# B-products of one state group moved from VectorE to GpSimd in the second layer's scans

## The chip, the cores and the metric

The kernel runs on one core of a Trainium2 chip. The metric is the device time of one execution in microseconds (us), from three runs of the kernel before: 15410.49 median, 15405.36 to 15414.3. A separate execution was recorded by the hardware profiler. The profile names the engines PE (TensorE, matrix products), DVE (VectorE), ACT (ScalarE), POOL (GpSimd) and SP (SyncE, which here only issues DMAs).

## The reference

Four layers run one after another on images of 64 x 64 tokens with 96 channels, four images in a batch. The first two are state-space layers with selective scans; the third (attention) and the fourth (Fourier mixing) and the feed-forward parts lie outside this change. The second layer's scan is, cut to what matters:

```python
def ss2d_core(xc, ...):                      # xc: 4 images, 192 channels, 4096 tokens
    xs = stack([x_hw, x_wh]); xs = concatenate([xs, flip(xs)])    # 4 directions
    dts, Bs, Cs = split(einsum(xs, x_proj_w), ...)                # 16 states
    delta = softplus(einsum(dts, dt_projs_w) + dt_projs_b)
    A = -exp(A_logs)
    def step(hst, inp):
        x_t, d_t, B_t, C_t = inp
        dA = exp(d_t[..., None] * A)
        hst = hst * dA + (d_t * x_t)[..., None] * B_t[:, :, None, :]
        y = einsum('bkdn,bkn->bkd', hst, C_t)
        return (hst, y)
    _, ys = scan(step, h0, seq)                                   # over 4096 tokens
```

So for every image, direction, channel and state there is one linear recurrence over 4096 tokens: the state is multiplied with a decay `dA` and the product `dt*x*B` is added. Then the states are weighted with `C` and summed. The first layer does the same with other scan orders (diagonals and radii), for which tokens are gathered.

## The kernel before, in words

**Tiling.** The 4096 tokens of a direction are cut into 4 segments of 1024. One image of one layer is a batch of 4 directions x 4 segments = 16 segments, which `Stream.batch` plans as one piece of work. Inside a segment the 192 channels x 16 states are cut into 24 groups: 6 channel blocks (`cb`) of 32 channels times 4 state groups (`sg`) of 4 states. A group is a tile of 128 partitions (32 channels x 4 states) by 1024 tokens.

**What happens to one group**, with the lines of the kernel before:
- `decay` (L1072, ScalarE): `da = exp(dts * A)`. `dts` is dt of the channel block, repeated over the states; it is loaded by a DMA that reads `dt_dram` with a broadcast (`load_dt`, L1056). `da` has 4 buffers in SBUF.
- `enter` (L1076, VectorE): `t = u * B`. `u` is dt*x of the channel block, repeated over the states by a matrix product into PSUM (`spread_u`, L1065, one buffer). `B` lies in SBUF in the tile `bc`, loaded per segment by broadcast DMAs (`load_states`, L1050). `t` has 2 buffers in PSUM.
- `recur` (L1083, VectorE): the scan, `h = da * h + t` along the tokens. `h` has 4 buffers in SBUF.
- `keep` (L1094, ScalarE): the last column of `h` is kept as the start of the next segment.
- `leave` (L1098, GpSimd): `hc = h * C`, with 3 buffers.
- `collect` (L1107, TensorE): sums `hc` over the states into PSUM; `keep_busy` (L1125) fills gaps of TensorE with products of zeros.

**Beside the groups** the planner lays the preparation of the next segment (`prepare`): tokens are transposed, projected to dt, B and C (L934, L947 to L951), dt goes through a softplus on ScalarE (an exponential and three passes, L991 to L995; the logarithm, L1006, with its table loads) and a sum on TensorE (L1014, L1017), is stored to `dt_dram` (L1020) and multiplied with x on GpSimd (`dtu`, L1023). B and C go through `bc_dram` (L981).

**What sets the order.** `batch` makes operations with an engine, a length, dependencies and due times, and `Flow.run` walks them once and emits each engine's instructions in a fixed order. Decay, product, scan and C-product are "hard": others may not be put before them if they would make them late. VectorE's order is written out: product, product, scan, scan for each pair of groups. Each engine then executes its instructions in order, waiting on semaphores, and SP issues the DMAs in order too, so a DMA that waits holds back those behind it.

**Between batches** `side_by_side` finishes an image (`merge`) while it prepares the next (`front`): these use temporaries `z_rows`, `xc`, `y_rows`, `yt`, `dx` and `halo`, taken from the pool `tmp` through `Rings`, a set of buffers that are taken and given back in turn.

Of the kernel before, what the change touches and what calls it, by code (L numbers as in the profile page):

```python
# [376 lines left out]
class Stream:  # L377
# [4 lines left out]
    def __init__(self, k, ctx, a, x, x1, y1):  # L382
# [20 lines left out]
        self.bc = k.t(w, [128, 2, NSG, SEG], "bc")  # L403
        self.zeros = k.t(w, [C, GC], "zeros")
        nc.gpsimd.memset(self.zeros, 0.0)

# [5 lines left out]
    def front(self, bt, plan, rings, first=None):  # L412
# [22 lines left out]
        def edges(s, st):  # L435

            halo = yield from take(self.tmp, [C, 2, HW], "halo", 2)
# [29 lines left out]
        def project(s, st):  # L467
# [31 lines left out]
            def outer(j):  # L499
# [6 lines left out]
                z = yield from take(self.tmp, [C, 2, CH], "z_rows", 2)  # L506
# [19 lines left out]
        def convolve(s, st):  # L526
            yield lambda: st.pad is not None
            xc = []
            for _ in range(C // GC):
                xc.append((yield from take(self.tmp, [128, CH], "xc", 3)))  # L530
# [26 lines left out]
            rows = yield from take(self.tmp, [128, 2, 4, DI], "y_rows", 1)  # L557
# [27 lines left out]
    def merge(self, bt, plan, rings):  # L585
# [29 lines left out]
        def times_d(n):  # L615

            x = yield from take(tmp, [128, T, DI], "dx", 1)
# [73 lines left out]
        def finish(n, acc, mv):  # L691
# [20 lines left out]
            yt = yield from take(tmp, [C, 2, CH], "yt", 1)  # L712
# [35 lines left out]
    def side_by_side(self, ahead, behind=None, flush=None, seg=None):  # L748
# [3 lines left out]
        plan, rings = Plan(), Rings(k)  # L752
        self.ended, self.idle = False, None
# [117 lines left out]
    def prepare(self, seg, base=0.0, before=None):  # L871
# [152 lines left out]

        for half in range(2):
# [17 lines left out]
            op(("u", half), "POOL", 2.31, partial(times, half), done, at=58.0 + 8.0 * half)  # L1043
# [13 lines left out]

    def spread_u(self, seg, cb):
# [10 lines left out]
    def decay(self, gr):  # L1069
        gr.da = self.k.t(self.core, [128, SEG], "da", bufs=4)  # L1070
        scale = gr.seg.bt.lay.neg_a[:, gr.seg.kd, gr.g : gr.g + 1]
        self.nc.scalar.activation(gr.da, gr.seg.dts[gr.cb], AF.Exp, scale=scale)  # L1072
# [5 lines left out]
    def recur(self, gr):  # L1078
# [6 lines left out]
        )  # L1085

# [97 lines left out]
    def batch(self, segs):  # L1184


        slot, length = 6.74, 6.74 * NCB * NSG / 2
        flow, last = Flow(self.keep_busy), segs[-1]
        add = flow.add
        groups = {}  # L1190
        dve = []
# [8 lines left out]
        for n, seg in enumerate(segs):  # L1200
            base, o, nxt = n * length, seg.o, seg.next
# [13 lines left out]
            for i in range(NG):  # L1215
                cb, sg = divmod(i, NSG)
                at = base + i // 2 * slot + i % 2 * 1.12
                gr = SimpleNamespace(seg=seg, cb=cb, sg=sg, g=i)
# [3 lines left out]
                if sg == 0:  # L1222
# [16 lines left out]
                    )  # L1239
                gr.decay = add(  # L1240
# [3 lines left out]
                    [o.get(("dts", cb)), of("recur", 4), of("decay", 1)],  # L1244
# [3 lines left out]
                gr.enter = add(  # L1248
                    "DVE",
                    1.115,  # L1250
                    partial(self.enter, gr),
                    [o["spread", cb], o.get(("load", 0, sg))],
                    lat=0.15,
                    due=at,
                    hard=True,
                )
                dve.append(gr)
# [1130 lines left out]
```

## Time and profile before

| what | value |
|---|---|
| median of three runs | 15410.49 us |
| the profiled execution's own time | 15402.95 us |
| its span, first to last instruction | 15401.2 us |
| granted TensorE clock, mean | 0.937 |
| VectorE busy over the span | 83% |
| GpSimd busy over the span | 60% |
| ScalarE busy over the span | 54% |
| second layer's batches and what lies between them, 6589 to 12195 us: VectorE / GpSimd / ScalarE busy | 5377 / 3936 / 3474 us of 5606 |

The page gives for each engine the busy time, then the span in 40 slices of 385 us with the busy share in tenths, then the costliest groups of instructions. A group's line reads: source line, engine, operation, tile written <- tiles read, shapes, count, then busy time and mean duration in ns, then how long the engine stood idle just before these instructions and which instruction's end released it. A timeline line reads: start, length, engine, line, operation, tiles, count of merged instructions, and in brackets the idle time before. Lines of waits read: who waited <- for whom: total us, times, longest.

### The profile page before, as it was taken

Reading aid. Unit: us, or ns where it says so; the run is one execution under the profiler, and the core shown is the slowest. Engines: PE = TensorE matmul, PEld = TensorE weight load, DVE = VectorE, ACT = ScalarE, POOL = GpSimd, SP = SyncE. Lnnn points to the kernel's source line nnn. Section 1 sums busy time; section 2 is a strip of 40 time slices with the busy share of each in tenths; the row PEclk is TensorE's granted clock in tenths of the full one; section 3 lists DMA queues with packets and bytes.
Section 4 is the critical chain, followed back from the end, with each engine's and each line's share of the span. In section 5 each row is a group of like instructions: output and inputs, shape, how many; then the busy total and the mean of one; then the engine's idle time right before and its main releaser. Section 6 shows DMA issues by size and latency. Waiting matters only on the chain. (4 is left out here: it accounts for less than half of the span.)

```text
span 15401.2 us, 196660 instructions
## 1 busy us (share of the span) xinstructions
PE 13827.4 (90%) x74369; PEld 5096.1 (33%) x74369; DVE 12827.4 (83%) x9642; ACT 8327.7 (54%) x13421; POOL 9203.3 (60%) x4657
## 2 busy tenths in 40 slices
PE   8899899989998999899989998999899789998877
PEld 3233333333333333333333333333233244443344
DVE  1999799978997899799979997999899856555655
ACT  3666466646664666466656665666566423232333
POOL 0788678867886688667747774777577620000123
PEclk9999899989998999899989999999999999998888
DMA  2333433343334333433343334333433400000122
GB/s 67 117 113 125 150 111 111 126 148 112 111 127 146 106 118 128 148 116 117 123 152 124 118 124 152 126 118 120 156 119 120 142 10 11 19 15 12 52 72 71
DMA packets 662768, 1637.49 MB, mean 106 GB/s; under 512 B 102822, under 2 KB 268460, under 8 KB 658045
## 3 DMA queue, kind: packets, MB, share of 16 engines
q1 hardware_dynamic: 624956, 1549.37, 31.4%
q0 software_dynamic: 36864, 75.55, 1.7%
q8 instruction: 588, 9.63, 0.3%
q14 instruction: 360, 2.94, 0.1%
HBM read 1295.03 MB, written 329.58 MB: 105 GB/s over the span
## 5 line engine op out<-in xcount | busy, mean ns | idle before, releaser
L1098 POOL TENSOR_TENSOR hc<-h,bc 128x1024 f32<-128x1024 f32 x3072 | 7198.4, 2365 | 2216.1 <-DVE h L1083 1909.0
L1083 DVE TENSOR_TENSOR_SCAN h<-da,state,t 128x1024 f32<-128x1024 f32 x2304 | 5300.4, 2355 | 26.0 <-ACT state L1094 16.3
L1072 ACT ACTIVATE da<-dts,L_A_logs 128x1024 f32<-128x1024 f32 x3072 | 3520.0, 1151 | 1832.2 <-DVE h L1083 1786.7
L1076 DVE TENSOR_TENSOR t<-u,bc 128x1024 f32<-128x1024 f32 x3072 | 3629.8, 1239 | 267.6 <-PE u L1065 193.5
L1107 PE MATMUL y<-hc,gather_y 128*32 128x512 f32 x12288 | 3529.1, 620 | 311.9 <-POOL hc L1098 241.7
L1125 PE MATMUL y<-L_diag,zeros 96*32 96x256 f32 x7824 | 1986.3, 386 | 0.0
L1083 DVE TENSOR_TENSOR_SCAN h<-da,t 128x1024 f32<-128x1024 f32 x768 | 1717.4, 2287 | 17.3 <-ACT da L1072 9.1
L1065 PE MATMUL u<-dtu,spread 32*128 32x512 f32 x3072 | 1573.1, 632 | 120.0 <-DVE t L1076 109.2
L1125 PEld LDWEIGHTS y<-L_diag,zeros 96*32 96x32 f32 x7824 | 852.8, 111 | 1425.0 <-issue 926.1
L1107 PEld LDWEIGHTS y<-hc,gather_y 128*32 128x32 f32 x12288 | 595.8, 109 | 2021.1 <-issue 1029.1
L934 PE MATMUL m<-xs,proj 96*128 96x512 f32 (+1 forms) x2048 | 1070.2, 641 | 67.3 <-ACT spare L1152 32.5
L1642 DVE SCALAR_TENSOR_TENSOR hcv<-padv,taps,hcv 128x2048 f32<-128x2048 f32 x384 | 902.2, 2350 | 13.4
L1566 POOL MEMSET padp<- 128x2448 f32 x32 | 68.6, 2143 | 1400.8 <-PE d L1606 1378.3
L1023 POOL TENSOR_TENSOR dtu<-dt,xs 96x1024 f32<-96x1024 f32 x256 | 603.0, 2356 | 506.1 <-ACT dt L1017 501.1
L1606 PE MATMUL d<-padp,diag 32*32 32x512 f32 x25600 | 885.7, 601 | 2.0 <-ACT hcp L1621 2.0
L1065 PEld LDWEIGHTS u<-dtu,spread 32*128 32x128 f32 x3072 | 521.4, 188 | 943.6 <-issue 588.0
L1017 ACT COPY dt<-m 96x512 f32<-96x512 f32 x512 | 297.2, 580 | 694.5 <-PE m L1014 690.0
L1014 PE MATMUL m<-dtu,ident 96*96 96x512 f32 x1024 | 563.8, 632 | 72.7 <-ACT dt L1017 65.9
L1606 PEld LDWEIGHTS d<-padp,diag 32*32 32x32 f32 x25600 | 484.4, 103 | 369.8 <-issue 196.9
L934 PEld LDWEIGHTS m<-xs,proj 96*128 96x128 f32 (+1 forms) x2048 | 324.6, 181 | 770.6 <-issue 483.8
L947 ACT ACTIVATE sp_z<-m,L_dtb 96x512 f32<-96x512 f32 x512 | 350.0, 684 | 409.5 <-PE m L934 393.5
L1014 PE MATMUL m<-sp_log,ident 96*96 96x512 f32 x1024 | 539.2, 608 | 0.0
(275 smaller groups left out, 15495.8 us busy)
## 6 DMA issues: line engine op xcount, KB each, us to landing
bc<-bc_dram SPq DMA_DIRECT2D x1024, 512.0 KB
dts<-dt_dram SPq DMA_DIRECT2D x768, 512.0 KB
dt_dram<-dt SPq DMA_DIRECT2D x256, 384.0 KB
y_tok<-spare SPq DMA_DIRECT2D x64, 768.0 KB
dt<-y_tok SPq DMA_DIRECT2D x128, 384.0 KB
x_tok<-y_rows SPq DMA_DIRECT2D x32, 768.0 KB
z_t<-z_rows SPq DMA_DIRECT2D x64, 384.0 KB
dx<-x_tok SPq DMA_DIRECT2D x64, 384.0 KB
```

Source lines behind the costliest of these rows:

```text
L934: nc.tensor.matmul(v.ps, seg.proj[:, src, to], seg.xs[:, src, chunks[j]], start=src == 0, stop=src == 1)
L1014: nc.tensor.matmul(v.ps, k.ident[:C, :C], term[:, half, chunks[j]], start=at == 0, stop=at == 3)
L1023: nc.gpsimd.tensor_mul(seg.dtu[:, half], v.dt[:, half], seg.xs[:, half])
L1065: self.nc.tensor.matmul(seg.u[:, cols], self.spread[rows, :], seg.dtu[rows, half, cols], start=True, stop=True)
L1072: self.nc.scalar.activation(gr.da, gr.seg.dts[gr.cb], AF.Exp, scale=scale)
L1076: self.nc.vector.tensor_mul(gr.t, gr.seg.u, self.bc[:, 0, gr.sg, :])
L1083: self.nc.vector.tensor_tensor_scan(gr.h[:, order], gr.da[:, order], gr.t[:, order], start, op0=ALU.mult, op1=ALU.add)
L1098: self.nc.gpsimd.tensor_mul(gr.hc, gr.h, self.bc[:, 1, gr.sg, :])
L1107: nc.tensor.matmul(seg.y[at : at + GC, :], self.gather_y, gr.hc[:, part * CH : (part + 1) * CH], start=gr.sg == 0, stop=gr.sg == NSG - 1, ...
L1125: self.nc.tensor.matmul(gr.seg.y[at : at + GC, :256], self.zeros, gr.seg.bt.lay.diag.rearrange("p h t c -> p (h t c)")[:, :256], start=Fal ...
L1606: nc.tensor.matmul(pc[i][j * 32 : (j + 1) * 32, :], diag[mine, ON_PE.index(t), tap, :], pad[mine, j * 8 + dy : j * 8 + dy + 8, dx : dx + H ...
L1642: nc.vector.scalar_tensor_tensor(to, win, wt, to, op0=ALU.mult, op1=ALU.add)
```

## The change

In the second layer (`lay.ordered` is false) the product with B of the third state group (`sg` = 2) in channel blocks 1 to 4 is computed by GpSimd. That is 4 of the 24 groups of a segment. GpSimd's operand is a copy of dt*x in SBUF: the preparation stores `dtu` to a DRAM tile `u_dram`, and a broadcast DMA (`load_u`) reads a channel block of it into a piece of a new SBUF tile `area`. GpSimd writes the product into another piece of `area` (`enter_pooled`). There are two pieces for copies and two for products. The decay of such a group is written by ScalarE into PSUM, into the buffer (tag `t`) that the group's own product would have taken; it is allocated behind the scan of the group two before. VectorE's order, which was product, product, scan, scan for all pairs, is product, scan, scan for a pair with such a group, and the due times follow that order. The decay of any other group now counts its 4 buffers over the groups that use them.

`area` has 7 x 1024 elements per partition. The temporaries of the stretches between batches named above become fixed pieces of it (`shared`), in the same rings.

```diff
+        self.area = k.t(w, [128, 7 * SEG], "area")
...
+        cut("z_rows", 2, C, h=2, t=CH)
+        cut("xc", 3, 128, t=CH)
+        cut("y_rows", 1, 128, f=2, t=4, d=DI)
+        cut("yt", 1, C, h=2, t=CH)
+        cut("dx", 1, 128, t=CH // 128, d=DI)
+        cut("halo", 2, C, e=2, w=HW)
...
-                z = yield from take(self.tmp, [C, 2, CH], "z_rows", 2)
+                z = yield from take(None, None, "z_rows", 2)
...
+        def u_out(half):
+            if half == 0:
+                seg.u_dram = k.t(self.dram, [2, C, SEG], "u_dram")
+            nc.sync.dma_start(seg.u_dram[half], seg.dtu[:, half])
...
+            if not lay.ordered:
+                op(("u_out", half), "SP", 0.1, partial(u_out, half), [p], at=60.0 + 8.0 * half, lat=3.0)
...
+    def load_u(self, gr):
+
+        gr.u = self.area[:, gr.pooled % 2 * SEG : (gr.pooled % 2 + 1) * SEG]
+        src = gr.seg.u_dram.rearrange("h c t -> (h c) t")[gr.cb * GC : (gr.cb + 1) * GC, :]
+        self.nc.sync.dma_start(gr.u, src.unsqueeze(1).to_broadcast([GC, GS, SEG]))
+
+    def enter_pooled(self, gr):
+        at = 2 + gr.pooled % 2
+        gr.t = self.area[:, at * SEG : (at + 1) * SEG]
+        self.nc.gpsimd.tensor_mul(gr.t, gr.u, self.bc[:, 0, gr.sg, :])
...
     def decay(self, gr):
-        gr.da = self.k.t(self.core, [128, SEG], "da", bufs=4)
+        if gr.pooled is None:
+            gr.da = self.k.t(self.core, [128, SEG], "da", bufs=4)
...
+        if gr.ahead:
+            gr.ahead.da = self.k.t(self.ps_t, [128, SEG], "t")
...
-        slot, length = 6.74, 6.74 * NCB * NSG / 2
+        pooled = lambda i: not segs[0].bt.lay.ordered and i % NSG == 2 and 0 < i // NSG < NCB - 1
+        order, times, at = [], {}, 0.0
+        for n in range(len(segs)):
+            for i in range(0, NG, 2):
+                order += [("enter", n, j) for j in (i, i + 1) if not pooled(j)]
+                order += [("recur", n, j) for j in (i, i + 1)]
+        for x in order:
+            times[x] = at
+            at += 1.12 if x[0] == "enter" else 2.25
...
+                if pooled(i):
+                    gr.pooled = len(theirs)
+                    theirs.append(gr)
+                    first = groups[n, i - 2]
+                    first.ahead, there = gr, [first.recur]
+                else:
+                    own.append(gr)
+                    there = [own[-5].recur] if len(own) > 4 else []
                 gr.decay = add(
                     "ACT",
                     1.05,
                     partial(self.decay, gr),
-                    [o.get(("dts", cb)), of("recur", 4), of("decay", 1)],
+                    [o.get(("dts", cb)), *there, of("decay", 1)],
...
+                if pooled(i):
+                    load = add(
+                        "SP",
+                        0.1,
+                        partial(self.load_u, gr),
+                        [theirs[-3].enter if len(theirs) > 2 else None, o.get(("u_out", cb // 3))],
+                        lat=4.5,
+                    )
+                    gr.enter = add(
+                        "POOL",
+                        2.31,
+                        partial(self.enter_pooled, gr),
+                        [load, o.get(("load", 0, sg)), theirs[-3].recur if len(theirs) > 2 else None],
+                        lat=0.2,
+                        hard=True,
+                    )
...
-        order = []
-        for j in range(0, len(dve), 2):
-            order += [dve[j].enter, dve[j + 1].enter, dve[j].recur, dve[j + 1].recur]
+        order = [groups[n, i].__dict__[kind] for kind, n, i in order]
```

## The prediction

> **What bounds the kernel now.** First the page: which engine is fullest, and where in the span.
>
> ```profile
> span 15401.2 us, 196660 instructions
> PE 13827.4 (90%) x74369; PEld 5096.1 (33%) x74369; DVE 12827.4 (83%) x9642; ACT 8327.7 (54%) x13421; POOL 9203.3 (60%) x4657
> ...
> DVE  1999799978997899799979997999899856555655
> ...
> POOL 0788678867886688667747774777577620000123
> ...
> L1098 POOL TENSOR_TENSOR hc<-h,bc 128x1024 f32<-128x1024 f32 x3072 | 7198.4, 2365 | 2216.1 <-DVE h L1083 1909.0
> L1083 DVE TENSOR_TENSOR_SCAN h<-da,state,t 128x1024 f32<-128x1024 f32 x2304 | 5300.4, 2355 | 26.0 <-ACT state L1094 16.3
> L1072 ACT ACTIVATE da<-dts,L_A_logs 128x1024 f32<-128x1024 f32 x3072 | 3520.0, 1151 | 1832.2 <-DVE h L1083 1786.7
> L1076 DVE TENSOR_TENSOR t<-u,bc 128x1024 f32<-128x1024 f32 x3072 | 3629.8, 1239 | 267.6 <-PE u L1065 193.5
> L1125 PE MATMUL y<-L_diag,zeros 96*32 96x256 f32 x7824 | 1986.3, 386 | 0.0
> ```
>
> VectorE is full in long stretches up to slice 32, broken by dips between batches. TensorE's 90% misleads: L1125 is its filler of zeros, and matmul ends are modelled. GpSimd and ScalarE idle mostly because they wait for VectorE's scan (1909 and 1787 us), so in the scans VectorE leads and the rest follow.
>
> Then the second layer alone. By the first product and the last scan in the timeline its four batches run from 6589 to 7891, 8051 to 9344, 9500 to 10801 and 10900 to 12195 us. First the waits of VectorE inside the first of them, then its timeline of two slots, then GpSimd's of the same kind:
>
> ```profile
> DVE t L1076 <- PE u L1065: 10.3, 15, 2.3
> DVE h L1083 <- ACT state L1094: 1.3, 1, 1.3
> ```
>
> ```profile
> 8504.72 2.38 DVE L1076 TENSOR_TENSOR t<-u,bc 128x1024 f32<-128x1024 f32 x2
> 8506.97 4.62 DVE L1083 TENSOR_TENSOR_SCAN h<-da,state,t 128x1024 f32<-128x1024 f32 x2
> 8511.46 2.39 DVE L1076 TENSOR_TENSOR t<-u,bc 128x1024 f32<-128x1024 f32 x2
> ```
>
> ```profile
> 8518.62 2.36 POOL L1023 TENSOR_TENSOR dtu<-dt,xs 96x1024 f32<-96x1024 f32 x1
> 8520.94 7.00 POOL L1098 TENSOR_TENSOR hc<-h,bc 128x1024 f32<-128x1024 f32 x3
> 8529.74 4.68 POOL L1098 TENSOR_TENSOR hc<-h,bc 128x1024 f32<-128x1024 f32 x2 [1.79 <-PE m L897]
> ```
>
> VectorE waits 11.6 us in 1290: it is the bound to 1%. Starts count here, not durations, which overlap by 0.12 us: two products take 8506.97 - 8504.72 = 2.25 us, so one is 1.125; two scans take 4.49; a slot of two groups is 6.74, and a segment of 12 slots 80.9. On GpSimd three in a row span 7.00, so one is (7.00 - 2.36) / 2 = 2.32 us. Its segment holds 24 C-products and 2 of dt*x, 26 x 2.32 = 60.3 us of 80.9: 20 us free.
>
> **The change, part by part.** The sum stands against the profiled execution, 15402.95 us (span 15401.2 and 1.8 around it); the median of the three runs, 15410.49, is 7.5 above, and I add that at the end.
>
> Removed: 4 products per segment on VectorE (third group of channel blocks 1 to 4), in 16 segments of 4 images: 256. In the new order the two scans of such a slot follow one product directly, so the slot is 6.74 - 1.125 = 5.62 and the segment 76.4. 256 x 1.125 = 288.0 us go if nothing else becomes late.
>
> Added on GpSimd: 4 products per segment from SBUF to SBUF, of L1098's shape, 2.32 us each. 30 x 2.32 = 69.6 us of 76.4: 6.8 us are left. Today GpSimd's waits in the first batch for things other than the scan (PE and dt copies) come to 56 us, 3.5 per segment; if all of that stays, 73.1 of 76.4. It fits, by 3.3 us. Its queue is in order, so I followed it by hand: in the built program the products of blocks 1 and 2 stand ahead of C-product 0 and 2, those of 3 and 4 ahead of C-product 8 and 12, each some 6 scans before its use (15 us or more). The two dt*x products stand after C-products 14 and 18, as close as GpSimd gets to its limit: from C-product 8 to 19 it has 15 products, 34.8 us, while VectorE passes 12 scans in 37.1. The C-product of scan 19 then ends about 5 us after that scan, and the h buffer it frees is wanted by scan 23, about 6 us later still. Cost 0.
>
> Moved on ScalarE: 256 decays write PSUM in place of SBUF. No row shows ScalarE writing PSUM. The nearest is L1072 itself, 1151 ns; below it L947, 683 ns for half as many elements out of PSUM; I take 1.15, bounds 1.0 to 1.4. What matters is the moment. Such a decay takes the PSUM buffer of the product two groups before it, so it can't start before that group's scan has ended; its own scan begins one scan and one product later, 2.25 + 1.125 = 3.37 us. Hand-off about 0.2, decay 1.15, hand-off 0.1: 1.45, slack 1.9. Behind it in ScalarE's order wait the next decays, which need no free PSUM. What can stand ahead of it: by the built order, in block 1 two halves of the softplus input and three 1.05 us passes, all behind the state copy of scan 3; these take about 5.0 us from 0.2 after that scan (13.7 us into the segment), so the decay starts at 18.7 and ends at 19.8, and scan 6 may start at 21.3. The logarithm (2 x 1.05 and two table loads of 1.28, 4.7 with gaps) stands behind block 2's decay and after it comes the decay of scan 13, at 40.9 for a start at 42.7. So 1.5 us of slack at the tightest. Taken: 0; if the decay is 0.3 slower it is still 0.
>
> Scan operands: a moved group reads the decay from PSUM and the product from SBUF, the other way round. L1076 is the row that has just that (u in PSUM, bc in SBUF) and keeps its 1.125 beside a busy GpSimd; L1083 without state, one operand fewer, takes 2.26 to 2.32 long. Taken 0, bounds -0.06 to +0.06 each, 15 us in all.
>
> A page of the Trainium skill speaks against the whole: "GPSIMD Engine Reference", section "Engine selection", sends elementwise products of two inputs to VectorE, GpSimd being about twice slower. By that rule each move costs 2.32 - 1.125 = 1.2 us of engine time, 306 us over 256. The rows agree on the ratio; but the same rows show 20 us per segment in which GpSimd only waits for VectorE, so here the rule has no price. A second rule bears on the PSUM decays: "SBUF — State Buffer", section "Who interferes with whom", says a VectorE instruction with two SBUF inputs and a GpSimd instruction reading SBUF block one another for a whole instruction. By it, a product in SBUF with a decay in SBUF would cost up to 2.32 us x 256; the change avoids that case, and no run here shows it yet.
>
> DMA and SP: per segment 2 stores of dt*x (as dt_dram, 384 KB each in the list) and 4 copies of 512 KB: 2.8 MB on top of 10.0 in the segment from 8504.6 to 8585.5. DMA is at 39% there; it goes to about 53%. Two fifths of that segment's slices move next to nothing, but for some 20 us, when the B and C loads come, the engines are 90% busy, and 1 MB more beside them takes 3 to 4 us at the 265 to 389 GB/s seen there. SP issues 6 more, half a microsecond each (L1056's 529 ns). Two of the copies stand behind the wait for their store's landing (L1056 waits up to 2.7 for dt_dram's today) and ahead of the next decay input dts, which by hand lands at 62 us of the segment and is needed at 67.6. The stores wait for GpSimd's dt*x, and the second stands ahead of the B loads of groups 1 to 3; the first of those is wanted 11 us later. Taken 0; if each such load came 1 us late at the block where slack ends, 64 us.
>
> Stretches between batches: temporaries now are pieces of one tile. Instruction order there is unchanged; about 100 ScalarE copies get a wait on ScalarE itself, 0 to 0.1 us each. 0 to 10; with the new start and end of four batches I put 8 us on all that is not in the sum.
>
> Sum: 15402.95 - 288 + 8 = 15123; plus 7.5 to the median: 15130 us.
>
> **Rivals.**
> Slower: GpSimd becomes the bound. A segment then takes 30 p + 3.5. At p = 2.32 it is 73.1; from p = 2.43 it is over 76.4 and eats the gain, from p = 2.58 (11% slower) it is over today's 80.9, and at p = 2.8 it is 87.5, 6.6 x 64 = 422 us slower: about 15830. For: only 3.3 us of room. Against: durations of L1098 lie between 2338 and 2407 ns beside a VectorE that never stops.
>
> Part given back: a decay in PSUM is late. If one of the four per segment is caught behind the logarithm, 4.7 - 1.9 = 2.8 us, 64 times: 179 of 288 lost, 15310. If the four lose 0.4 each: 102 lost, 15232. For: all other decays may run ahead by 4 buffers, these by none; ScalarE waited up to 4.6 us for TensorE (L947) in the first batch. Against: the hand count above.
>
> Nothing: TensorE is the true bound, and VectorE's gap moves into waits for u (L1065). 15410. For: 94% busy in these batches. Against: a fifth of that is filler, and VectorE waited 10.3 us for it in 1290.
>
> **Chances and range.** Gain of about 265 to 295: 0.71. Part given back, gain 31 to 265: 0.17, mostly in its upper half. No change: 0.04. Slower: 0.08. A measurement tells about 0.2%, 31 us. Faster 0.88, same 0.04, slower 0.08. The range goes from 15100 (scans 0.06 faster, no residue) to 15260, where the late-decay case with 0.4 to 0.5 us each lies; that holds the likeliest case and some 0.1 of the second.
>
> **What would show it.** Right: second-layer L1083's slots at 5.6 us in blocks 1 to 4, segments of 76.4, VectorE still without idle time, the new product on GpSimd at about 2.36 x256, GpSimd above 90% in these batches. Wrong: scans of these groups waiting for ScalarE (late decay), for GpSimd (product or a freed h), a product row well above 2.4, or B loads late at segment starts.

## The result and the profile after

| | kernel before | changed kernel |
|---|---|---|
| median | 15407.92 us (15374.57 to 15414.3, 4 runs) | 15613.17 us (15588.92 to 15632.09, 4 runs) |
| profiled execution, span | 15401.2 us | 15587.1 us |
| second layer's batches, first to last product | 1296, 1288, 1295, 1289 us | 1347, 1351, 1350, 1342 us |
| segment in the steady part of a batch | 80.9 us | 85.0 us |
| granted TensorE clock in these batches | 0.98 to 0.99 | 0.90 to 0.91 |

The ratio is 1.0137, with a 95% interval of 1.0116 to 1.0157: 205 us slower, where 280 us faster was forecast. The four batches took some 55 us more each, 222 in all, so they hold the whole loss: the rest of the profiled execution was 36 us shorter than before. The page of the changed kernel, with the lines that answer to those of the kernel before (L1125 is the scan, L1118 VectorE's product, L1142 the C-product, L1169 the filler of zeros; new is L1097, the product on GpSimd):

```profile
span 15587.1 us, 193930 instructions
...
DVE  1999799969997999699979997999899855655555
...
PEclk9999899989998999889889898898889899998888
...
L1142 POOL TENSOR_TENSOR hc<-h,bc 128x1024 f32<-128x1024 f32 x3072 | 7193.4, 2362 | 1422.3 <-DVE h L1125 1201.1
L1125 DVE TENSOR_TENSOR_SCAN h<-da,state,t 128x1024 f32<-128x1024 f32 x2112 | 4843.1, 2333 | 26.4 <-ACT state L1138 14.7
...
L1118 DVE TENSOR_TENSOR t<-u,bc 128x1024 f32<-128x1024 f32 x2816 | 3319.0, 1222 | 555.1 <-PE u L1106 473.5
...
L1169 PE MATMUL y<-L_diag,zeros 96*32 96x256 f32 x6090 | 1563.3, 388 | 0.0
...
L1097 POOL TENSOR_TENSOR area<-area,bc 128x1024 f32<-128x1024 f32 x256 | 602.2, 2352 | 183.9 <-DMA area<-u_dram 123.5
```

The moved product takes 2352 ns and the C-product is as fast as before. VectorE's idle time before its products doubled, from 267.6 to 555.1 us, and it waits for TensorE. The clock row of the kernel before was

```profile
PEclk9999899989998999899989999999999999998888
```

It read 9 from slice 22 to 36; now seven of the slices 22 to 32, in the second layer, read 8. VectorE's waits in the second layer alone (us in total, times, longest):

```profile
DVE t L1118 <- PE u L1106: 320.6, 118, 7.0
DVE h L1125 <- ACT t L1114: 185.0, 62, 3.4
```

In the kernel before the first of these was smaller in the same stretch, and the second did not exist:

```profile
DVE t L1076 <- PE u L1065: 46.0, 32, 7.0
```

About 460 us of new waits stand against 288 us of products that went. VectorE's timeline shows both waits, and between them that the shorter slot is real:

```profile
8512.44 2.35 DVE L1125 TENSOR_TENSOR_SCAN h<-t,state,area 128x1024 f32<-128x1024 f32 x1 [2.85 <-ACT t L1114]
...
8523.80 1.23 DVE L1118 TENSOR_TENSOR t<-u,bc 128x1024 f32<-128x1024 f32 x1
8524.94 2.34 DVE L1125 TENSOR_TENSOR_SCAN h<-t,state,area 128x1024 f32<-128x1024 f32 x1
8527.20 2.32 DVE L1125 TENSOR_TENSOR_SCAN h<-da,state,t 128x1024 f32<-128x1024 f32 x1
8529.44 1.21 DVE L1118 TENSOR_TENSOR t<-u,bc 128x1024 f32<-128x1024 f32 x1
```

```profile
8559.48 2.36 DVE L1118 TENSOR_TENSOR t<-u,bc 128x1024 f32<-128x1024 f32 x2 [4.10 <-PE u L1106]
```

From 8523.80 to 8529.44 is 5.64 us, the slot that was forecast. The segment begins at 8488.0. In block 1 the moved scan waits 2.85 us for its decay, in block 5 the first product waits 4.10 us for u. With 0.76 us for u of block 4, and four times 0.12 us where a product now follows the scan whose buffer it takes, these are 8.2 of the 8.6 us between 85.0 and 76.4. The means over eleven steady segments of this batch are much the same: 3.04 us for the decay of block 1, 0.56 and 4.04 for u of blocks 4 and 5.

Both waits lead to TensorE, which executes in order. Its timeline at the first one (L1192 transposes y, L957 is the projection for the next segment, L1106 the u of block 1, L1151 collects):

```profile
8493.95 0.66 PE L1192 MATMUL m<-ident,yc 128*128 128x128 f32 x4 [1.56 <-ACT dt L972]
8495.55 2.08 PE L957 MATMUL m<-xs,proj 96*128 96x512 f32 x2 [0.94 <-ACT spare L1196]
8497.56 3.78 PE L1106 MATMUL u<-dtu,spread 32*128 32x512 f32 x4
8501.26 3.63 PE L1151 MATMUL y<-hc,gather_y 128*32 128x512 f32 x8
8504.82 1.36 PE L957 MATMUL m<-xs,proj 96*128 96x512 f32 x2
```

The windows there (us, busy time and instructions of PE, PEld, DVE, ACT, POOL, then the granted clock, DMA share and GB/s), and what stands behind the projection in ScalarE's order:

```profile
8496.00:8500.00 4.00, 4.00 (x5) 1.21 (x5) 4.00 (x3) 0.82 (x3) 4.00 (x3) 0.50 1.05 192
8500.00:8504.00 4.00, 4.00 (x10) 0.56 (x8) 4.00 (x4) 0.19 (x1) 3.01 (x3) 0.50 0.88 315
```

```profile
8506.22 0.68 ACT L970 ACTIVATE sp_z<-m,L_dtb 96x512 f32<-96x512 f32 x1 [4.41 <-PE m L957]
...
8511.24 1.10 ACT L1114 ACTIVATE t<-dts,L_A_logs 128x1024 f32<-128x1024 f32 x1
```

After 1.56 and 0.94 us of waiting the clock is at half, and u takes 3.78 us where it takes 1.98 at full clock. At their lengths at full clock, shown by other rows of this segment (1.13, 1.98, 1.91 and 1.12 us), the four rows from the projection to the projection would be 4.7 us shorter; that is an estimate. The second half of the projection ends 18.2 us into the segment; ScalarE has waited 4.41 us for it, and the decay, which would have to start at 20.4 for its scan to begin in time at 21.6, starts at 23.2. At the second wait:

```profile
8553.85 1.10 PE L1037 MATMUL m<-dtu,ident 96*96 96x512 f32 x2
8554.79 1.02 PE L1037 MATMUL m<-sp_z,ident 96*96 96x512 f32 x2
8555.65 1.02 PE L1037 MATMUL m<-dt,ident 96*96 96x512 f32 x2
8556.51 1.02 PE L1037 MATMUL m<-sp_log,ident 96*96 96x512 f32 x2
8557.46 1.98 PE L1106 MATMUL u<-dtu,spread 32*128 32x512 f32 x4
```

L1037 is the softplus sum of the next segment, four terms of about 0.9 us for each of four pieces. The u that VectorE needs at 8555.3 stands behind the fourth sum. The first and the last term in the same segment of the kernel before, which begins at 8457.6, and the first term here:

```profile
8489.14 1.10 PE L1014 MATMUL m<-dtu,ident 96*96 96x512 f32 x2
...
8516.90 1.02 PE L1014 MATMUL m<-sp_log,ident 96*96 96x512 f32 x2
```

```profile
8537.16 1.10 PE L1037 MATMUL m<-dtu,ident 96*96 96x512 f32 x2
```

In the kernel before the sums start 31.6 us into the segment and end at 60.4; here they start at 49.1 and end at 69.5.

### The profile page after: what moved, and what is told of

Same layout as the page of the kernel before. It is cut to its first block, busy times and chain, and to the rows that moved or that the text cites. A ratio compares the mean times of both kernels' runs of the same rounds, so it can differ in the third digit from the quotient of the medians.

```text
span 15587.1 us, 193930 instructions
## 1 busy us (share of the span) xinstructions
PE 13841.2 (89%) x72635; PEld 4989.3 (32%) x72635; DVE 12590.8 (81%) x9386; ACT 8272.4 (53%) x13421; POOL 9774.2 (63%) x4913
## 5 line engine op out<-in xcount | busy, mean ns | idle before, releaser
L1142 POOL TENSOR_TENSOR hc<-h,bc 128x1024 f32<-128x1024 f32 x3072 | 7193.4, 2362 | 1422.3 <-DVE h L1125 1201.1
L1125 DVE TENSOR_TENSOR_SCAN h<-da,state,t 128x1024 f32<-128x1024 f32 x2112 | 4843.1, 2333 | 26.4 <-ACT state L1138 14.7
L1151 PE MATMUL y<-hc,gather_y 128*32 128x512 f32 x12288 | 3683.3, 653 | 172.8 <-POOL hc L1142 148.2
L1118 DVE TENSOR_TENSOR t<-u,bc 128x1024 f32<-128x1024 f32 x2816 | 3319.0, 1222 | 555.1 <-PE u L1106 473.5
L1114 ACT ACTIVATE da<-dts,L_A_logs 128x1024 f32<-128x1024 f32 x2816 | 3205.2, 1147 | 871.7 <-DVE h L1125 832.7
L1106 PE MATMUL u<-dtu,spread 32*128 32x512 f32 x3072 | 1723.7, 685 | 348.6 <-DVE t L1118 333.0
L1125 DVE TENSOR_TENSOR_SCAN h<-da,t 128x1024 f32<-128x1024 f32 x704 | 1571.1, 2271 | 12.0 <-ACT da L1114 8.8
L1169 PE MATMUL y<-L_diag,zeros 96*32 96x256 f32 x6090 | 1563.3, 388 | 0.0
L957 PE MATMUL m<-xs,proj 96*128 96x512 f32 (+1 forms) x2048 | 1171.0, 680 | 188.3 <-ACT dt L972 120.6
L1151 PEld LDWEIGHTS y<-hc,gather_y 128*32 128x32 f32 x12288 | 622.6, 113 | 2025.4 <-issue 1103.8
L1169 PEld LDWEIGHTS y<-L_diag,zeros 96*32 96x32 f32 x6090 | 658.3, 112 | 1152.3 <-issue 776.8
L1106 PEld LDWEIGHTS u<-dtu,spread 32*128 32x128 f32 x3072 | 555.4, 200 | 1338.8 <-issue 991.5
L1097 POOL TENSOR_TENSOR area<-area,bc 128x1024 f32<-128x1024 f32 x256 | 602.2, 2352 | 183.9 <-DMA area<-u_dram 123.5
L957 PEld LDWEIGHTS m<-xs,proj 96*128 96x128 f32 (+1 forms) x2048 | 326.2, 190 | 925.0 <-issue 478.6
L1037 PE MATMUL m<-dtu,ident 96*96 96x512 f32 x1024 | 563.1, 632 | 32.4 <-ACT dt L1040 26.2
```

The costliest lines, as they stand in the source:

```text
L957: nc.tensor.matmul(v.ps, seg.proj[:, src, to], seg.xs[:, src, chunks[j]], start=src == 0, stop=src == 1)
L1097: self.nc.gpsimd.tensor_mul(gr.t, gr.u, self.bc[:, 0, gr.sg, :])
L1106: self.nc.tensor.matmul(seg.u[:, cols], self.spread[rows, :], seg.dtu[rows, half, cols], start=True, stop=True)
L1118: self.nc.vector.tensor_mul(gr.t, gr.seg.u, self.bc[:, 0, gr.sg, :])
L1125: self.nc.vector.tensor_tensor_scan(gr.h[:, order], gr.da[:, order], gr.t[:, order], start, op0=ALU.mult, op1=ALU.add)
L1142: self.nc.gpsimd.tensor_mul(gr.hc, gr.h, self.bc[:, 1, gr.sg, :])
```

## Experiments

Three theories. **A, the clock**: TensorE's gaps drop the clock, and that makes projections and sums late. **B, order and load**: the planner now puts the preparation of the next segment later in TensorE's order, and TensorE has too little room behind it. **C, fillers**: they are placed where the plan has a gap, and where TensorE runs behind the plan each one is a delay. The kernel before took 15245 to 15408 us in the different sets, so every run is compared by its ratio to the kernel before in its own set; a second measurement of the changed kernel gives the same ratio as the first:

> The changed kernel as it is, once more beside the kernel before, since the kernel before took 15249 us on the chip of the first four experiments against 15408 us on the one of the result: it gives the ratio that the other runs of this set are held against. Expected: 1.0137 as in the result, within 0.003.

Measured: 1.0141 (1.0125 to 1.0158), as in the result.

**Fillers across the ends of the blocks.**

```diff
-                stop=gr.sg == NSG - 1,
+                stop=gr.sg == NSG - 1 and (part == 1 or seg.bt.lay.ordered),
...
     def copy_y(self, seg):
+        self.close(10)     # eleven zero products, the last closes the group
```

> The changed kernel; in the second layer the accumulation group of a channel block stays open until the next block's first collect or the copy of y, so that fillers can run in TensorE's two idle gaps of about 3 us at the blocks' ends (ten are put directly ahead of the copy of y). Theory A (the gaps drop TensorE's clock to 0.5 for 8 to 9 us twice a segment, and that makes the projections and sums, and through them the decays in PSUM and the late u, late): the granted clock in the second layer's batches rises from 0.90 to 0.96 or more, VectorE's waits for the PSUM decay (185 us) and for u (321 us) fall below half, and the time comes to 15200 to 15400. Theory B (the order of the chain projection - ScalarE - sums, not the clock, leaves no slack at the shorter segment): the clock rises, the waits stay within a third, and the time stays above 15520.

Measured: 1.0564. The granted clock in the batches rose from 0.90 to between 0.93 and 0.96. A's time is missed; B has the clock and the time, which stays above its bound, but not the waits: those for u rose to 794 us. Of the two stretches at half clock in a segment of the changed kernel, 10.2 and 6.8 us in most, one is gone. The other stayed: the eleven products of zeros (4.9 us) only moved the gap behind them, the transposes still waited 1.26 us and the projection 0.76 to 0.94, and the clock fell to 0.50 there. As the products themselves delay the projection, the run gives no fair test of A; it shows what fillers ahead of the projection cost.

**No fillers, in the kernel before and in the changed one.**

```diff
-        if gr is None:
+        if gr is None or not gr.seg.bt.lay.ordered:
             return
```

> The kernel before with no filler matmuls in the second layer's batches (they add zeros and pad TensorE's short gaps). Theory A: the granted clock there falls from 0.98 to 0.7 or less, the projections and sums come late although no product was moved, VectorE shows the waits for u that the changed kernel shows, and the time rises from 15408 to 15550 or more. Theory B: the clock falls, but at a segment of 80.9 us the chain has the slack for it, and the time stays below 15460.

Measured: 1.0022 (1.0012 to 1.0031). One window of the kernel before, then the same for the run without fillers:

```profile
8200.00:9200.00 1000.00, 937.97 (x3203) 309.49 (x3202) 1000.00 (x597) 655.43 (x950) 755.58 (x323) 0.99 0.39 126
```

```profile
8200.00:9100.00 900.00, 777.67 (x2185) 211.43 (x2184) 895.37 (x534) 582.66 (x850) 676.41 (x290) 0.90 0.38 122
```

The clock falls to 0.90, just what the changed kernel has, and the price is 33 us. A low clock alone does not make the loss as long as the segment has room. The run also takes the fillers' own time from TensorE, so the price of the clock by itself is not isolated, and it does not say what the same clock costs in a segment of 76.4 us.

> The changed kernel without the filler matmuls of the second layer (442 in 1100 us, 0.22 us of TensorE's queue each at full clock, some 7 us a segment). Theory A (clock): the granted clock falls below 0.90, the decay in PSUM and the u come later still, and the time rises by 0.3% or more. Theory B (the preparation of the next segment, projections and sums through one PSUM bank, is a loop that the shorter segment leaves no room for): the fillers stand where TensorE waits anyway, so the time stays within 0.3%. Theory C (the fillers are placed by gaps in the plan, and where TensorE runs behind the plan each is a plain delay ahead of collects, sums and spreads): the waits for u (321 us) fall by 100 us or more, and the time falls by 0.6 to 1.5%.

Measured: 1.0040 (1.0026 to 1.0055), 1.0% below the changed kernel at the same granted clock of 0.90. Its waits:

```profile
DVE t L1118 <- PE u L1106: 197.0, 73, 7.0
DVE h L1125 <- ACT t L1114: 169.4, 63, 3.7
```

The waits for u fell by 115 us, against 312 in the second measurement of the changed kernel, as C has it. The wait for the decay hardly moved, so C is a part and not the whole.

**The fourth group in place of the third**, with a wider window for the decay in PSUM.

```diff
-        pooled = lambda i: ... i % NSG == 2 and 0 < i // NSG < NCB - 1
+        pooled = lambda i: ... i % NSG == NSG - 1 and 0 < i // NSG < NCB - 1
...
-                    first = groups[n, i - 2]
+                    first = groups[n, i - 3]
```

> The changed kernel with the fourth state group of blocks 1 to 4 moved in place of the third: VectorE's order becomes product, product, scan, scan, product, scan, scan, and a decay in PSUM may start right after the scan three before its own, a window of 5.6 us in place of 3.4. Both theories: the wait of 185 us of the moved scans for the decay in PSUM goes (below 40 us). Theory A: the decay was late because of the clock and the u of blocks 4 and 5 too, so the waits for u stay near 320 us: 15613 - 185 x (0.8 to 1) = 15430 to 15465. Theory B: what VectorE no longer waits in block 1 it waits later, for u, which stands behind the sums in TensorE's order: 15520 to 15613.

Measured: 1.0050 (1.0033 to 1.0067), 0.9% below the changed kernel. The wait for the decay fell from 181 to 31 us; the waits for u stayed, 292. In ratios A had 1.0014 to 1.0037 and B 1.0073 to 1.0133, so neither is met; the run only shows that the two waits are largely separate.

> The fourth group moved in place of the third (1.0050 of the kernel before), and no filler matmuls in the second layer. A: above 1.008. B: 1.002 to 1.008. C: the 279 us of waits for u fall below 150 us, and the ratio to 0.990 to 0.998, faster than the kernel before.

Measured: 0.9988 (0.9979 to 0.9998). Between the numbers of B and C: the waits for u fell from 292 to 198 us, not below 150.

**Decays in SBUF again.**

```diff
-        if gr.pooled is None:
-            gr.da = self.k.t(self.core, [128, SEG], "da", bufs=4)
+        gr.da = self.k.t(self.core, [128, SEG], "da", bufs=4)
```

> The changed kernel with the moved groups' decays in SBUF again, in the ring of four that every group had before: the window of the decay is as in the kernel before, and the moved scan reads both operands from SBUF. Theories A and B as for the fourth group: the 185 us of waiting for the decay in PSUM goes, and the time is 15430 to 15465 (A) or 15520 to 15613 (B). Where two SBUF operands slow the scan against GpSimd's reads of SBUF, the moved scan lasts longer than its 2340 ns: 256 x 0.25 us per 10% are 64 us on top.

Measured: 1.0136, and the reason is neither A nor B. The groups of most of its second layer (6600 to 12250 us):

```profile
L1124 DVE TENSOR_TENSOR_SCAN h<-da,state,t 128x1024 f32<-128x1024 f32 x935 | 2142.3, 2322 | 0.0
...
L1124 DVE TENSOR_TENSOR_SCAN h<-da,state,area 128x1024 f32<-128x1024 f32 x188 | 810.3, 4310 | 0.0
...
L1097 POOL TENSOR_TENSOR area<-area,bc 128x1024 f32<-128x1024 f32 x246 | 579.4, 2355 | 122.9 <-DMA area<-u_dram 122.9
```

The waits are gone (41 us left for u), but a scan with both operands in SBUF lasts 4310 ns beside GpSimd, against 2343 with the decay in PSUM: some 500 us over 256. Single scans took 3.2 to 6.4 us. GpSimd's own products did not slow (2355); of its C-products in the second layer three took 4.4 us, none in the changed kernel over 2.41. So the PSUM decays of the change are no ornament; and with the longer scans, in segments of 84.3 us, VectorE hardly waits.

**Less work in the sums.** One term of four, then two, then two in the kernel before.

```diff
-                for term in range(4):
+                for term in range(0 if lay.ordered else 2, 4):   # two terms
```

> The changed kernel with one of the four terms of each softplus sum in the second layer: the log term alone is added, the terms of the rounding remainder, of z and of the positive part are left out, so that TensorE has 12 matmuls of 0.93 us fewer per segment (11 us). Theory B: the loop of projections and sums gets 11 us of room, sums end by 60 us into the segment, the waits for u and for the decay in PSUM all but go (below 80 us of 506), and the time is what was predicted for the change: 0.980 to 0.986. Theory A: the idle gaps and the clock of 0.90 stay, with them half or more of the waits: 0.995 or above. Theory C: the fillers stay in the queue, but with 11 us less work TensorE is no longer behind the plan: as B.

Measured: 0.9831 (0.9815 to 0.9847).

> The changed kernel with two of the four terms of each softplus sum in the second layer, the positive part and the log: the two that hold what is lost in rounding 1 + z are left out. TensorE has 8 matmuls fewer per segment (7.4 us of 14.8). Load theory, and the loop through the one PSUM bank: with 7.4 us less the sums end by 62 us into the segment and the batches come to 1225 to 1245, ratio 0.983 to 0.988. Clock theory: the idle gaps at the ends of odd blocks stay and the ratio stays above 0.995.

Measured: 0.9835 (0.9812 to 0.9857), 15127.68 us against 15383.27. Its waits in the second layer, a window and two slots of its VectorE:

```profile
DVE t L1119 <- PE u L1107: 40.1, 18, 7.0
DVE h L1126 <- ACT t L1115: 12.9, 7, 3.2
```

```profile
8200.00:9100.00 900.00, 830.36 (x2755) 262.49 (x2754) 895.74 (x516) 609.59 (x890) 819.16 (x353) 0.94 0.51 164
```

```profile
8134.45 1.23 DVE L1119 TENSOR_TENSOR t<-u,bc 128x1024 f32<-128x1024 f32 x1
8135.59 2.34 DVE L1126 TENSOR_TENSOR_SCAN h<-t,state,area 128x1024 f32<-128x1024 f32 x1
8137.85 2.32 DVE L1126 TENSOR_TENSOR_SCAN h<-da,state,t 128x1024 f32<-128x1024 f32 x1
8140.08 2.34 DVE L1119 TENSOR_TENSOR t<-u,bc 128x1024 f32<-128x1024 f32 x2
```

VectorE is full again, the segment is 76.9 us, and GpSimd is busy for 91% of the window, and VectorE waits 0.9 us for it in the whole layer's scans. The ratio is what the prediction said of the change itself, 15130 / 15410 = 0.982. But fewer terms also led the planner to another order: the first sum starts at 30.3 us here and at 30.8 with one term, against 49.2 (medians of steady segments). So these two runs change load and order together.

> The kernel before with the same two terms left out in the second layer, and nothing moved. VectorE sets its segment of 80.9 us and nothing in it waits for TensorE: 0.997 to 1.002. Where it gains more than 0.3%, part of the gain of the run with two terms is not the change's.

Measured: 1.0017 (1.0007 to 1.0028). The lighter sums gain nothing by themselves. The planner rearranged this kernel too, with the sums 2 to 31 us into the following segment, so it is no control for the order; but in the batches of the kernel before all waits for u were 46 us, 0.3%, so its VectorE had little to get back. The gain of 1.65% is that of the moved products.

**Order alone.** The due times of the preparation 8 us earlier; in the first four runs the shift also took the first layer, which shares `prepare` (8.0 there too).

```diff
+        early = 0.0 if lay.ordered else 8.0
...
-            at = 20.0 + 3.5 * (2 * half + j)
+            at = 20.0 - early + 3.5 * (2 * half + j)
```

> The changed kernel, third group and fillers as they are; only the due times of the preparation of the next segment are 8 us earlier (projections, ScalarE's softplus, log, sums), which makes the planner put the second projection ahead of the transposes of y and the first sum ahead of the fourth u instead of behind the eleventh collect. Nothing is added or left out. Theory B (an order laid out too late, the loop through one PSUM bank): the sums start near 32 us into the segment instead of 49, the waits for u (321 us) and for the decay in PSUM (185 us) fall below 150 together, and the ratio falls from 1.0141 to 0.983 to 0.995. Theory C (fillers are the delay, whatever the order): the ratio stays above 1.004, the one without fillers.

> As the run with the due times 8 us earlier, and no filler matmuls in the second layer. B: with an order that has room, fillers cost nothing or little: within 0.3% of the run with fillers. C: 0.5% or more faster than that one. Theory A (clock): slower than that one by 0.3% or more, as the granted clock falls further.

> The fourth group in place of the third, due times 8 us earlier, no fillers in the second layer: all three at once. B and C both expect the whole of what the removed products are worth: segments of 76.4 to 77.5 us, ratio 0.980 to 0.987, faster than the kernel before and at or below the run with one term of the sums (0.9831). A: above 0.992.

> The kernel before with the same due times 8 us earlier and nothing else. B: its segment of 80.9 us is set by VectorE and the preparation has room in it, so an earlier order gains nothing: 0.998 to 1.002. If it gains 0.5% or more, the earlier order would be a gain of its own and not the cover that the change lacked.

Measured: 1.0070, 1.0128, 1.0149 and 1.0118. B's numbers missed in all of them. C's holds for the first (above 1.004) and misses in the second and third; A's hold for the second and third. The last shows why the ratios can't be used as they are: the first layer's batches rose from some 1333 to some 1370 us with the shift, about 150 us, the larger part of the 1.2% that the kernel before loses. Its second layer's batches also take 58 us more than in the profile of the kernel before, so there the earlier order gains nothing. Inside the second layer they still tell something. With fillers the batches fell from 1348 to 1285 us, without them they were 1305, at a clock of 0.86 to 0.87 in the batches against 0.94: with the earlier order fillers help, and here the clock of theory A has a price. The early fourth group without fillers stayed at 1308.

> The run with the due times 8 us earlier also shifted the first layer's batches, which share the function: they took 1370 us each against 1333 in the changed kernel, some 150 us that are no part of the question. Here the shift holds for the second layer alone, with the third group and the fillers of the changed kernel. The second layer's batches were 1285 us with the shift against 1348 without, 4 x 63 = 250 us. Order theory (the late place of projections and sums in TensorE's order is the larger part of what was lost): ratio 1.0141 - 0.016 = 0.996 to 1.000. Load theory (TensorE has too much work for a segment of 76.4 us wherever the sums stand): the batches stay above 1330 and the ratio above 1.010.

Measured: 0.9974 (0.9962 to 0.9986), faster than the kernel before with all the work of the change in it. Granted clock 0.94. Its waits:

```profile
DVE h L1126 <- ACT t L1115: 161.1, 65, 5.4
DVE t L1119 <- PE u L1107: 83.3, 117, 7.0
```

The first sum now starts at 30.1 us and the last ends at 63; the waits for u fell from 312 to 83. The late decay has only changed its place, from block 1 to block 3 (2.4 us a segment; the expectation of the run with the fourth group, below, says block 4), where ScalarE stands behind the copies of the sums.

**The same order at another clock.** The traces of this run and of the second measurement of the changed kernel hold a comparison that no run was made for. In each, some segments have the instructions of all four engines in the same order and take different times. Two such segments of the second measurement, first their windows (the granted clock is the third number from the end), then VectorE's waits in the first and in the second:

```profile
8025.30:8106.00 80.70, 74.13 (x232) 22.89 (x230) 77.03 (x46) 52.68 (x82) 69.93 (x31) 0.94 0.49 161
8442.90:8527.90 85.00, 77.03 (x231) 23.34 (x230) 77.08 (x45) 52.53 (x82) 69.80 (x31) 0.90 0.47 153
```

```profile
DVE t L1118 <- PE u L1106: 1.8, 1, 1.8
DVE h L1125 <- ACT t L1114: 1.7, 1, 1.7
```

```profile
DVE t L1118 <- PE u L1106: 4.9, 2, 4.1
DVE h L1125 <- ACT t L1114: 2.9, 1, 2.9
```

TensorE's first instructions are alike to 0.2 us until the projection 7.4 us into the segment. Then the clock is at half for 6.8 us in the first and 10.2 in the second; the projection's second half ends at 17.0 against 18.2 us, the decay is waited for 1.7 against 2.9 us, the first sum starts at 44.8 against 49.2. And two of the run with the earlier order:

```profile
8160.80:8238.30 77.50, 74.22 (x248) 23.88 (x246) 76.92 (x46) 52.89 (x82) 69.92 (x31) 0.98 0.51 168
8795.30:8877.20 81.90, 78.62 (x248) 24.73 (x246) 77.12 (x45) 52.79 (x82) 70.05 (x31) 0.92 0.48 157
```

In that run, leaving out each batch's first and last segment, those with 3.4 us at half clock take 76.5 to 77.5 us, with 6.8 us 78.1 to 79.1, with 10.2 us 79.0 to 80.7 and with 13.7 us 81.7 to 81.9. So with all four terms of the sums and the earlier order the whole of the forecast gain is there in the segments where the clock drops only briefly, and about half of the 8.6 us lost in a segment of the changed kernel goes with the length of the stretches at half clock. This is a comparison inside two runs: longer waits of TensorE also drop the clock, and no run set the clock by itself.

> The changed kernel with only channel blocks 2 and 3 moved (128 of the 256 products): VectorE's segment falls by 2.25 us to 78.6 in place of 4.5. If TensorE's preparation bounds the segment, at 80 to 82 us with this planner, the dose does not matter below that: the waits are smaller, the time lies at 1.000 to 1.006, slower than before all the same. If the waits grew with each moved product (GpSimd's share, the decays in PSUM), half the dose gives half the loss: 1.007. If the segment were VectorE's again, 16 x 2.25 x 4 = 144 us faster: 0.991.

Measured: 1.0094 (1.0073 to 1.0114). Half the products moved lose two thirds of what all of them lose, and inside the batches nearly all of it (1338 to 1341 us, against 1338 to 1351 in the second measurement of the changed kernel): the waits for u are there in full (323 us), those for the decay nearly gone (17 us). None of the three numbers is met. That the loss does not follow the dose fits the first of them in kind, and B, since here too the first sum starts late, at 48.4 us; the granted clock is 0.89.

**All together.**

> All four terms of the sums, the fillers, and the due times 8 us earlier in the second layer alone (0.9974 with the third group), with the fourth group moved in place of the third. What is left in the run with the third group is 2.5 us a segment in which the moved scan of block 4 waits for its decay in PSUM. If the narrow window of 3.4 us causes it, the window of 5.6 us takes 1.5 to 2.5 us of it away: 64 x 2 = 130 us, ratio 0.988 to 0.993. If ScalarE is late there whatever the window, because it stands behind the copies of the sums, the wait moves to the next u or decay: 0.995 to 1.000.

Measured: 1.0015 (1.0003 to 1.0027), a miss. The wait for the decay fell from 161 to 65 us, and the waits for u rose from 83 to 188, mostly for block 4's u behind the first sums (2.2 us a segment). Here what was taken away in front of this stretch of TensorE came back at its next handover.

> The fourth group moved, two of the four terms of the sums (positive part and log) in the second layer, and ScalarE without the four passes that make the two terms left out (4.2 us a segment). The run with the third group and the two terms has segments of 76.9 us, 0.5 from VectorE's own 76.4, so little is left: 0.980 to 0.985. Above 0.986 only if the waits inside the pairs of the fourth group (0.13 us, four a segment, 33 us) count in full.

Measured: 0.9873 (0.9856 to 0.9889): a miss upwards, and slower than the third group with two terms. Of the kernels tried, that one (0.9835) is the fastest that still computes the softplus, if the two terms that hold the rounding remainder of 1 + z may go; with all four terms it is the earlier order (0.9974).

## Why the prediction was wrong, step by step

- **Removed, 288 us.** Right: slots of 5.64 us, and 76.9 us a segment where VectorE does not wait.
- **Added on GpSimd, 0.** Right: 2352 ns against the 2.32 us taken, and VectorE never waits for a moved product in steady segments. In the run with two terms GpSimd is at 91% with all products done in time. The rival that GpSimd becomes the bound is wrong, and the rule of the Trainium skill weighed there ("GPSIMD Engine Reference", "Engine selection") had no price here, as argued.
- **Decays in PSUM, 0.** The length was right (1.10 us against 1.15), the moment wrong. The hand count followed ScalarE's order alone and let block 1's decay start 18.7 us into the segment; it started at 23.2, because ScalarE's passes ahead of it waited for TensorE's second projection, which ends at 18.2. The forecast's rival "part given back" had the right kind of wait, and its size (179 us for one decay of four caught behind the logarithm, 185 measured) agrees by luck: the decay that was late was another, for another reason.
- **Scan operands, 0.** Right: 2343 ns with the operands swapped, 2329 without. The second rule, "SBUF — State Buffer", "Who interferes with whom", fits the run that has what the change avoids: 4310 ns with both in SBUF, an addition of 1.97 us where the bound was 2.32. No run has such a scan beside an idle GpSimd.
- **DMA and SP, 0.** Right: GpSimd waited for its copy three times in four batches (123.5 us, longest 49.9), at batch starts, and VectorE for no load of B in the scans.
- **Stretches between batches, 8.** Right in size: the three in the second layer took 420 us against 414.
- **The step that failed is one that the sum does not have: TensorE.** Its in-order queue was not followed in the built kernel. The argument against the rival "TensorE is the true bound" (chance 0.04), that VectorE waited only 10.3 us for it in 1290, told of segments of 80.9 us. In the changed kernel the last sum ends at 69.5 us and u of block 5, wanted 67 us into the segment, stands behind it: 4.10 us of the 8.6 lost there, and 320.6 us of waits for u in all (46.0 before), where the sum has nothing. That rival was the nearest in mechanism, though its 15410 was too kind: the waits are not a limit that takes back the gain but an order that costs more than the gain.
- The removed fillers (7824 to 6090 on the page) could have been a sign before the run: the built kernel had fewer gaps in TensorE's plan.

What made the loss, as far as the runs show it: the late place of the preparation in TensorE's order, and the stretches at half clock that TensorE's gaps bring with them. The order alone, with nothing left out, gives 1.7% (1.0141 to 0.9974). At one and the same order, the segments with less time at half clock lose 4 to 5 us less. Half of the sums' work away, which also brings the sums forward, gives the whole forecast gain (0.9835). Fillers, by the late order, cost 1.0% and 0.6%; by the early order and in the kernel before they gain. The clock is no cause by itself: at 0.90 the kernel before, whose segment has room, loses 0.2%. No run held the clock at full in the changed kernel, so how the loss divides between order and clock is not shown; by the estimate above the half clock can account for the whole wait for the decay of block 1. Open is why the planner's order tips so early, at half the dose already, and what would keep TensorE's gaps, and with them the last 3 to 5 us a segment, out of the version with the earlier order.

## What to carry to other kernels

When the bounding engine's period is cut, every engine's in-order queue has to be walked again at the new period, also the ones that only wait a little today: small waits at the old period say nothing on the slack at the new one. Where a planner lays out the order, look in the built kernel at where the longest chain of the background work (here projection, softplus, sums) now starts and ends, and at what stands behind its last piece. Padding that was placed for planned gaps can be a delay when the real engine runs behind the plan: here it cost 0.6 to 1.0% by the late order and gained by the early one. And where segments of one run with the same order take different times, comparing them can separate a cause that no experiment has isolated.

## What the hardware showed that was not expected

- Scans on VectorE with both big operands in SBUF took 4310 ns (4529 without a start state) in the mean beside a GpSimd that reads SBUF most of the time, against 2343 (2282) with one of them in PSUM. GpSimd's products kept their 2355 ns; but for three C-products of 4.4 us the loss falls on VectorE.
- TensorE's clock went to 0.50 at 8495.1, 2.7 us after the end of the last collect, with 0.66 us of transposes between, and came back at 8505.3. The Trainium skill, "TensorE: Matmul & The Clock Gate", Part 1, has half rate after an idle window of about 3.4 us; here a shorter stretch, with transposes in it, was enough. The stretches at half clock in the steady segments read here lasted 3.4, 6.8, 10.2 or 13.7 us, multiples of 3.41: TensorE worked again from 8495.6, and the clock was still at half for 9.8 us.
- In the kernel before, without fillers, a granted clock of 0.90 in place of 0.98 to 0.99 cost only 0.2%; in the changed kernel two segments of the same order differ by 4.3 us at 0.94 and 0.90.
